# Text exponentials of four heads as one instruction, with subtraction and sum on the vector engine, in a two-layer cross-attention

## The chip, the cores and the metric

The kernel runs on one core of a Trainium2 chip. The metric is the device time of one execution in microseconds (us). The kernel before took 2083.08 us, the median of three runs (2079.56, 2083.08 and 2083.56).

The core's engines are called by the profile's names: PE does matrix products and transposes (PEld is its loading of weights), DVE is the vector engine, ACT the scalar engine (exponentials and scaled copies), POOL the general one, and SP only issues DMA transfers. PE's results land in PSUM, a small memory of banks; the other operands lie in SBUF, the core's working memory.

## The reference, cut to what matters

Two cross-attention layers are computed one after the other. The second takes the first's result as its `x`. Everything is in fp32.

```python
# x: (8, 100, 640); ctx: (8, 722, 1024) = 77 text tokens, then 645 ip tokens; 20 heads of 32
text, ip = ctx[:, :77], ctx[:, 77:]
q = x @ Wq;  k, v = text @ Wk, text @ Wv;  k_ip, v_ip = ip @ Wk_ip, ip @ Wv_ip
# layer 0: attention over the text tokens and, apart from it, over the ip tokens
out = softmax(q k^T * scale) v + softmax(q k_ip^T * scale) v_ip
# layer 1: the ip scores get a term that is the same for all heads, and the ip part a mask by query
text_probs = softmax((q @ k^T over all 640 channels) * scale)
sem = ((text_probs @ text) @ ip^T) * scale
out = softmax(q k^T * scale) v + mask * (softmax(q k_ip^T * scale + 0.5 * sem) v_ip)
# both layers
x = out @ Wo + bo + x
```

There are two softmaxes for each query and head: one over 77 text scores and one over 645 ip scores. The change touches how the first is computed.

## The kernel before, in words

**The first stage (L222 to L407).** It loads x (`xt`, two batches at a time) and the query weights of layer 0 (`wq0`, five pieces of 128 rows) on SP's queue (L227 to L233). It multiplies them (`psq`, L253: four groups of two batches, k outermost, five products of 128x200 for each k; the trace counts two PE instructions for each fp32 product of the code) and then makes the text keys and values of both layers (`text_k`, `text_v`, `text_v_blocks`). These come from a scheme of seven products of half-size blocks for eight (`seven`). It needs sums of blocks of the tokens (`token_sums`: two on DVE at L213 and L214, two on POOL at L215 and L216) and of the weights (`weight_sums`). The tile `s_text` holds the token sums of the text, and `sums` names which block or sum each of the seven products reads. Results go to device memory by DMA on POOL's queue.

**The main stage.** The work is cut into 16 units u (8 batches of layer 0, then 8 of layer 1), taken in pairs. A unit has five chunks c of four heads each; `ORDER` lists the 80 chunks, in the last pair with the two units' chunks mixed. In each chunk PE does, in an order written by hand (`manual_schedule`, the loop at the end of the kernel):

1. the scores against the first 512 keys (`scores`, part 0, L837),
2. transposes j = 0 and 1 of the chunk before (`transposes`, L922), then 2 and 3,
3. the scores against the remaining 210 keys, 133 of ip and 77 of text (part 1),
4. transposes 4 and 5 of the chunk before, then its product with the values (`values`, L944).

Between these stand fillers. They make keys and values of later pairs (`pair_tasks`, `two_chunks`, `fifth_chunk` with products `psk` L669 and `psv` L675), or the output product and layer 1's query product of a finished pair (`out_piece` L752, `q_piece`). `production` puts each filler at a place on a time axis of chunks, from a start and an end (`plan`) and a cost; `spread` levels them; `between` makes all fillers due before a point. Before each small piece, and at each such point, `apart` also pulls one filler forward that would be due within the next 0.4 of a chunk. `fifth[1]` are six half products of three v blocks for the last pair; the plan spreads them from n + 6.9 to n + 8.6, where n = 70 is the first chunk of that pair. At the very end, in chunk 79, `last_out` multiplies the output weights for the last two units (`pso_last`, L804), adds the residual on DVE (L811) and stores.

**The softmax of a chunk (`scores`).** The scores of four heads lie in one PSUM tile `sc`, which has one buffer, so the next scores product waits until all have read it. DVE takes maxima (L846 in layer 0; L853 in layer 1, which adds `sem` and writes the sum to `p`). ACT takes exponentials with the sums of their rows (L861; each is followed by a read of the accumulator). For the text part, `text_maxima` takes the four heads' negated maxima in one DVE instruction (L867), and `text_exponentials` has ACT do one exponential per head over 77 elements, straight from `sc`, with the maximum as bias and the row sum in the accumulator (L875). DVE makes factors (L878 to L883), ACT scales the first 512 columns of p (L889), DVE scales the rest (L893 and L897). The transposes then read p, two at a time, since their PSUM tiles (`ps_pt`, shared with the output products) have two buffers. Copies to SBUF free them: j = 2 and 5 on ACT (L927), the others on DVE (L929).

These steps are put off in a list `later` and emitted one by one between fillers. An entry marked True has to be emitted before the next scores product, because it reads `sc`. The order on the engines other than PE is the scheduler's.

**Small weights.** `load_wo` (L740 to L743) loads five pieces of 320 KB for the output product ("o"), and in layer 0 five more for the query product ("q"), into tiles tagged "wo" with two buffers, on SP's queue. The pieces are used by `out_piece` in the second chunk of the following pair: two ahead of the first transposes, and one at each of the three later places. A load can start when the piece two before it has been used. `out_piece` adds bias and residual on DVE (L757).

Of the kernel before, what the change touches and what calls it, by code (L numbers as in the profile page):

```python
# [9 lines left out]
F32 = mybir.dt.float32  # L10
AF = mybir.ActivationFunctionType
ALU = mybir.AluOpType
AX = mybir.AxisListType

P = 128
B = 8
S = 100
C = 640
CC = 1024
NT = 77  # L20
# [24 lines left out]
def two_layer_xattn(  # L45
# [166 lines left out]
    def token_sums(a11, a12, a21, a22, s1, s2, s3, s4):  # L212
        nc.vector.tensor_tensor(s1, a21, a22, ALU.add)  # L213
        nc.vector.tensor_tensor(s2, s1, a11, ALU.subtract)  # L214
        nc.gpsimd.tensor_tensor(s3, a11, a21, ALU.subtract)  # L215
        nc.gpsimd.tensor_tensor(s4, a12, s2, ALU.subtract)  # L216
        return {1: a11, 2: a12, 3: s4, 4: a22, 5: s1, 6: s2, 7: s3}
# [4 lines left out]
    with ExitStack() as es:  # L222
        fp = es.enter_context(tc.tile_pool(name="first", bufs=1))
        pj.append(es.enter_context(tc.tile_pool(name="ps_first", bufs=6, space=PSUM)))
        xt = fp.tile([P, B, NC_, S], F32, tag="x", name="xt")
        wq0 = []
        nc.sync.dma_start(xt[:, :2], x_t[:, :2])  # L227
        for k in range(NC_):
            t = fp.tile([P, C], F32, tag="wr", name=f"wq0_{k}", bufs=NCC)
            nc.sync.dma_start(t, wq[0][k * P : (k + 1) * P, :])  # L230
            wq0.append(t)
# [15 lines left out]
        for g in range(B // 2):  # L247
# [16 lines left out]
                )  # L264
            nc.gpsimd.dma_start(q_d[0][g], t)

        st = fp.tile([P, 4, HK, TH], F32, tag="s", name="s_text")
        sums = token_sums(
            *(text[:, HK * h : HK * (h + 1), TH * i : TH * (i + 1)] for i in range(2) for h in range(2)),
            *(st[:, i] for i in range(4)),  # L270
        )

        def text_k(l):
            t = fp.tile([P, 2, 512], F32, tag="ev", name=f"kt4_{l}", bufs=2)
# [110 lines left out]
        def sums_of(kind):  # L385
            weight_sums(kind, {"v": HC, "k": 2 * P}[kind], (nc.vector, nc.gpsimd))

        with tc.manual_schedule(engines={mybir.EngineType.PE}):
            sums_of("k")
            text_k(0)  # L390
            load_wk(wkt[1])
            text_v(0)
            sums_of("v")
            load_left(0)
            text_v_blocks(0)
            load_wv(wvt[1])
            sums_of("k")
            text_k(1)
            load_wk(wki[0])
            left_v(0)  # L400
            load_left(1)
            left_text()
            text_v(1)
            sums_of("v")
            text_v_blocks(1)
            sums_of("k")
            left_v(1)  # L407
# [331 lines left out]

    def load_wo(kind, src, g):  # L740
        for c in range(NC_):
            t = wpool.tile([P, NC_, P], F32, tag="wo", name=f"{kind}_{g}_{c}", bufs=2)
            nc.sync.dma_start(t, src.rearrange("(k p) n -> p k n", p=P)[:, :, c * P : (c + 1) * P])  # L743
            wos[kind, g, c] = t

# [52 lines left out]
    def last_out(i, ks_):  # L798
        g = len(PAIRS) - 1
        if ks_[0] == 0:  # L800
            last_ps[i] = product_ps(f"pso_last_{i}")
        for k in ks_:
            for c in range(NC_):
                nc.tensor.matmul(  # L804
                    last_ps[i][:, c * S : (c + 1) * S], lhsT=last_w[c][:, k, :], rhs=hsg[g][:, i, k, :],
                    start=(k == 0 and c == 0), stop=(k == NC_ - 1), skip_group_check=True,
                )
        if ks_[-1] < NC_ - 1:
            return
        r = resg[g][:, i].rearrange("p c s -> p (c s)")  # L810
        nc.vector.tensor_tensor(r, last_ps[i][:, : NC_ * S], r, ALU.add)  # L811
        nc.sync.dma_start(out[LAST[i] % B], resg[g][:, i])
# [14 lines left out]
    def scores(u, c, part):  # L827
# [38 lines left out]
        def text_maxima():  # L866
            nc.vector.tensor_reduce(st[:, 2, :], sc[:S, :, n:KB], AX.X, ALU.max, negate=True)  # L867

            nc.vector.tensor_tensor(lo, st[:, 0, :], st[:, 1, :], ALU.min)
            nc.vector.tensor_tensor(f, lo.unsqueeze(1).to_broadcast([S, 2, 4]), st[:, 0:2, :], ALU.subtract)  # L870

        def text_exponentials():
            nc.scalar.activation(f, f, AF.Exp)
            for i in range(4):
                nc.scalar.activation(  # L875
                    p[:, i, NI:], sc[:S, i, n:KB], AF.Exp, bias=st[:, 2, i : i + 1], accum_out=st[:, 5, i : i + 1]
                )
            nc.vector.tensor_tensor(st[:, 3:5, :], st[:, 3:5, :], f, ALU.mult)  # L878
            nc.vector.tensor_tensor(st[:, 4, :], st[:, 3, :], st[:, 4, :], ALU.add)

# [21 lines left out]
        if part == 0:  # L902
            maxima((0, 1))
            later.append((True, lambda: (exponentials((0, 1)), maxima((2, 3)))))
            later.append((True, lambda: exponentials((2, 3))))
        else:
            maxima((0, 1, 2, 3))
            later.append((True, lambda: (exponentials((0, 1, 2, 3)), text_maxima())))
            later.append((True, text_exponentials))
            later.append((False, lambda: (factors(), scaled((0, 1)), scaled_rest(False))))  # L910
            later.append((False, lambda: (scaled((2, 3)), scaled_rest(True))))

    pts = {}

    def transposes(u, c, j):
        if j == 0:
            emit(len(later))
            pts[u, c] = one.tile([P, 6, 4 * S], F32, tag="pt", name=f"pt_{u}_{c}")
        rows = P if j < 5 else NTAIL
        ps = ps_pt.tile([P, 512], F32, tag="pt", name=f"pspt_{u}_{c}_{j}")  # L920
        for i in range(4):
            nc.tensor.transpose(  # L922
                ps[:rows, i * S : (i + 1) * S], pr[u, c][:, i, j * P : j * P + rows], ident[:S, :S]
            )
        dst, src = pts[u, c][:rows, j, :], ps[:rows, : 4 * S]
        if j % 3 == 2:
            nc.scalar.copy(dst, src)  # L927
        else:
            nc.vector.tensor_copy(dst, src)  # L929
# [27 lines left out]
    def production():  # L957
# [18 lines left out]
        ]  # L976
        plan.append((n - 10 - AHEAD, n + 2.9, by_chunks[0] + by_chunks[1]))
        plan.append((n + 2.9, n + 6.9, fifth[0]))
        plan.append((n + 6.9, n + 8.6, fifth[1]))
        return [task for a, b, tasks in plan for task in spread(a, b, tasks)]  # L980

    def spread(a, b, tasks):
# [91 lines left out]
    with tc.manual_schedule(engines={mybir.EngineType.PE}):  # L1074
# [20 lines left out]
        def apart(until):  # L1095

            while done[0] < len(todo) and todo[done[0]][1] < until and not any(
                t for t, _, _ in todo[mark[0] : done[0]]
            ):
                next_task()  # L1100
            mark[0] = done[0]

        def between(n, a, b, small):

            mark[0] = done[0]
            for i, (_, f) in enumerate(small):
                make(n + a + (b - a) * (i + 1) / (len(small) + 1))
                apart(n + b + 0.4)
                f()
            make(n + b)  # L1110
            apart(n + b + 0.4)

        make(0.0)
        last = None
# [29 lines left out]
            last = (u, c)  # L1144
        last_out(0, [NC_ - 1])
        for j in range(6):
            transposes(*last, j)
        values(*last)
        last_out(1, [NC_ - 1])


# [44 lines left out]
```

## Time and profile before

| what | value |
|---|---|
| median of three runs | 2083.08 us |
| profiled execution, its own time | 2088.13 us |
| profiled execution, its span | 2086.4 us |
| mean clock granted to PE | 0.996 |
| DVE busy, instructions | 988.3 us, 2526 |
| ACT busy, instructions | 862.8 us, 2830 |
| ACT, text exponentials L875: busy, mean of one | 99.5 us, 320 ns |
| ACT, their accumulator reads: busy, mean of one | 64.2 us, 201 ns |

The span runs from the first to the last instruction of the profiled execution; its own time has 1.7 us more around it, and this execution took 5.05 us more than the median. In a list of groups, a row names a line, an engine, an operation, output and inputs, the shape, the count, then busy time and mean duration in ns, then the engine's idle time ahead of it and what ended that. In a timeline, a row gives start and duration of a run of equal instructions, and in brackets how long the engine had been idle and who released it. In a table of windows, each row is a stretch of time with each engine's busy time, PE's granted clock as a share of full speed, the DMA share and GB/s. A busy PE is not a PE at full speed: at half clock it counts as busy too.

### The profile page before, as it was taken

Reading aid. Unit: us, or ns where it says so; the run is one execution under the profiler, and the core shown is the slowest. Engines: PE = TensorE matmul, PEld = TensorE weight load, DVE = VectorE, ACT = ScalarE, POOL = GpSimd, SP = SyncE. Lnnn points to the kernel's source line nnn. Section 1 sums busy time; section 2 is a strip of 40 time slices with the busy share of each in tenths; the row PEclk is TensorE's granted clock in tenths of the full one; section 3 lists DMA queues with packets and bytes.
Section 4 is the critical chain, followed back from the end, with each engine's and each line's share of the span. In section 5 each row is a group of like instructions: output and inputs, shape, how many; then the busy total and the mean of one; then the engine's idle time right before and its main releaser. Section 6 shows DMA issues by size and latency. Waiting matters only on the chain. (4 is left out here: it accounts for less than half of the span.)

```text
span 2086.4 us, 41767 instructions
## 1 busy us (share of the span) xinstructions
PE 2058.5 (99%) x16690; PEld 1641.6 (79%) x16690; DVE 988.3 (47%) x2526; ACT 862.8 (41%) x2830; POOL 379.8 (18%) x409
## 2 busy tenths in 40 slices
PE   8999999999999999999999999999999999999998
PEld 8676787777777777787788877887888778889786
DVE  2111221345554554444464554445455455667565
ACT  1001000245434544344444544445444445566576
POOL 3213211111110111111141111111111113223120
PEclk9999999999999999999999999999999999999999
DMA  9345232323333443352544443353344344545482
GB/s 350 108 134 165 87 87 78 113 75 96 103 99 119 119 118 88 96 162 81 157 121 131 124 117 81 103 156 94 85 112 132 104 122 136 158 119 142 126 227 73
DMA packets 299104, 255.58 MB, mean 123 GB/s; under 512 B 43102, under 2 KB 267794, under 8 KB 298910
## 3 DMA queue, kind: packets, MB, share of 16 engines
q1 hardware_dynamic: 279374, 184.48, 32.6%
q0 software_dynamic: 19536, 68.43, 9.8%
q8 instruction: 132, 2.16, 0.4%
q14 instruction: 62, 0.51, 0.1%
HBM read 183.93 MB, written 68.93 MB: 121 GB/s over the span
## 5 line engine op out<-in xcount | busy, mean ns | idle before, releaser
L861 ACT ACTIVATE p<-sc,st 100x512 f32<-100x512 f32 (+1 forms) x320 | 166.5, 528 | 227.3 <-DVE st L846 227.3
L929 DVE COPY pt<-pspt 128x400 f32<-128x400 f32 x320 | 175.9, 569 | 122.4 <-PE pspt L922 119.4
L861 ACT ACTIVATE p<-p,st 100x512 f32<-100x512 f32 (+1 forms) x320 | 177.0, 555 | 134.9 <-DVE st L853 134.5
L889 ACT ACTIVATE p<-p,st 100x512 f32<-100x512 f32 x320 | 209.6, 714 | 48.6 <-DVE st L883 48.2
L922 PE MATMUL pspt<-ident,p 100*128 100x100 f32 (+1 forms) x1920 | 212.2, 251 | 7.2 <-DVE res L757 2.5
L922 PEld LDWEIGHTS pspt<-ident,p 100*128 100x128 f32 (+1 forms) x1920 | 187.8, 138 | 37.2 <-issue 5.5
L528 PE MATMUL psv_a<-wv,x 128*128 128x397 f32 (+1 forms) x560 | 185.3, 473 | 2.0 <-ACT vo L174 2.0
L927 ACT COPY pt<-pspt 128x400 f32<-128x400 f32 (+1 forms) x160 | 77.9, 487 | 254.8 <-PE pspt L922 254.7
L528 PE MATMUL psv_d<-wv,s 128*128 128x320 f32 (+1 forms) x560 | 174.7, 454 | 0.0
L552 POOL DMA_DIRECT2D v_d<-vo x70 | 39.5, 564 | 723.6 <-DVE gst L520 386.4
L846 DVE TENSOR_REDUCE st<-sc 100x2 f32<-100x1024 f32 (+1 forms) x120 | 126.2, 1052 | 68.2 <-ACT p L861 37.8
L528 PEld LDWEIGHTS psv_a<-wv,x 128*128 128x128 f32 x560 | 103.1, 189 | 65.9 <-issue 9.4
L853 DVE CUSTOM_DVE_ANT_0 p<-sc,sem 100x512 f32<-100x512 f32 (+1 forms) x320 | 139.6, 490 | 25.4 <-PE sc L837 25.3
L528 PEld LDWEIGHTS psv_d<-wv,s 128*128 128x128 f32 x560 | 103.6, 190 | 56.0 <-issue 6.6
L536 PEld LDWEIGHTS psk_a<-x,wk 128*128 128x128 f32 x1120 | 132.3, 191 | 12.7 <-issue 9.4
L837 PE MATMUL sc<-k,q 32*100 32x210 f32 (+1 forms) x1280 | 140.6, 509 | 1.2 <-ACT p L861 0.6
L564 POOL DMA_DIRECT2D k_d<-ko x70 | 58.2, 831 | 448.6 <-DVE ko L200 426.6
L536 PE MATMUL psk_d<-s,wk 128*128 128x128 f32 (+1 forms) x1120 | 139.7, 277 | 0.0
L536 PE MATMUL psk_a<-x,wk 128*128 128x128 f32 (+1 forms) x1120 | 139.1, 277 | 0.0
L536 PEld LDWEIGHTS psk_d<-s,wk 128*128 128x128 f32 x1120 | 131.2, 191 | 8.2 <-issue 3.3
L503 PE MATMUL psk<-x,wk 128*128 128x256 f32 (+1 forms) x560 | 131.6, 383 | 0.0
L503 PEld LDWEIGHTS psk<-x,wk 128*128 128x128 f32 x560 | 102.1, 189 | 23.2 <-issue 7.9
(207 smaller groups left out, 3403.5 us busy)
## 6 DMA issues: line engine op xcount, KB each, us to landing
x<-ip_t SPq DMA_DIRECT2D x84, 512.0 KB
k<-k_d SPq DMA_DIRECT2D x80, 322.5 KB
v<-v_d SPq DMA_DIRECT2D x80, 320.0 KB
v_d<-vo POOLq DMA_DIRECT2D x70, 320.0 KB, 2.6
k_d<-ko POOLq DMA_DIRECT2D x56, 320.0 KB, 6.8
x<-ip_t SPq DMA_DIRECT2D x22, 532.0 KB
o<-wo SPq DMA_DIRECT2D x35, 320.0 KB
q<-wq SPq DMA_DIRECT2D x20, 320.0 KB
```

What stands on the lines that cost most here:

```text
L503: nc.tensor.matmul(ps[:, : 2 * n], lhsT=W["k", 4][:, k, :], rhs=xs[j][:, :, k, :n], start=(k == 0), stop=(k == NCC - 1),)
L528: nc.tensor.matmul(ps[:, :m], lhsT=sums[which][:, k, :P], rhs=w[:, k, :], start=(k == 0 and not go_on), stop=(k == HK - 1), skip_group_che ...
L536: nc.tensor.matmul(ps[:, r * n : (r + 1) * n], lhsT=W["k", WHICH[which]][:, k, r * P : (r + 1) * P], rhs=sums[which][:, k, :], start=(r == ...
L564: nc.gpsimd.dma_start(k_d[u][:, :, n0 : n0 + n], ko[0][:, h, :, :n])
L837: nc.tensor.matmul(sc[:S, i, : k1 - k0], lhsT=qs_[u][rows, c, :], rhs=ks[u, c][rows, k0:k1], start=True, stop=True)
L846: nc.vector.tensor_reduce(st[:, part, heads[0] : heads[-1] + 1], sc[:S, heads[0] : heads[-1] + 1, :n], AX.X, ALU.max, negate=True,)
L853: nc.vector.tensor_tensor_reduce(out=p[:, i, k0 : k0 + n], in0=sc[:S, i, :n], in1=sems[u][:, k0 : k0 + n], scale=-1.0, scalar=3.0e38, op0= ...
L861: nc.scalar.activation(dst, dst if l else sc[:S, i, :n], AF.Exp, bias=st[:, part, i : i + 1], scale=-1.0 if l else 1.0, accum_out=st[:, 3 ...
L889: nc.scalar.activation(p[:, i, :KA], p[:, i, :KA], AF.Copy, scale=mul[:, 0, i : i + 1])
L922: nc.tensor.transpose(ps[:rows, i * S : (i + 1) * S], pr[u, c][:, i, j * P : j * P + rows], ident[:S, :S])
L927: nc.scalar.copy(dst, src)
L929: nc.vector.tensor_copy(dst, src)
```

## The change

1. **Text softmax.** `text_maxima` has one more DVE instruction: it adds the negated maxima to the text scores of the four heads and writes them to `p`. `text_exponentials` is one exponential over the 4 x 77 elements in SBUF, without a sum, and one sum on DVE. Its entry in `later` is False now: it no longer reads `sc`.
2. **Small weights.** The "wo" tiles have three buffers.
3. **Plan of the last products.** `fifth[1]` is spread to n + 8.95. From chunk 76 on, `apart` looks 0.1 of a chunk ahead.
4. **The end.** Transposes j = 0 of the last chunk are copied by ACT. The addition and the store of `last_out` are a function of their own, called after the last transposes in the program's text.
5. **The start.** The first two batches of x are loaded in five pieces (128 x 2 x 100, 100 KB each), each ahead of the query weights of the same k. `s_text` takes the place of `xt`, so the text's token sums, now made after the weight sums, wait for the last `psq` product.

By the instruction order of the two programs, PE's order differs only in the last chunks. The half products of the fifth chunks (`psk`, `psv`) there are, by chunk: before, 3 in chunk 76, 4 in 77 and none in 78; after, 2 in 76, 3 in 77 and 2 in 78. In chunk 76 the first transposes now come before the half product that they stood behind. On SP's queue three "o" loads stand together where two did, and the following two come one place later.

```diff
@@ -222,10 +222,12 @@
     with ExitStack() as es:
         fp = es.enter_context(tc.tile_pool(name="first", bufs=1))
         pj.append(es.enter_context(tc.tile_pool(name="ps_first", bufs=6, space=PSUM)))
-        xt = fp.tile([P, B, NC_, S], F32, tag="x", name="xt")
+        xt = fp.tile([P, 4 * HK * TH], F32, tag="x", name="xt")[:, : B * NC_ * S].rearrange(
+            "p (b k s) -> p b k s", b=B, k=NC_
+        )
         wq0 = []
-        nc.sync.dma_start(xt[:, :2], x_t[:, :2])
         for k in range(NC_):
+            nc.sync.dma_start(xt[:, :2, k], x_t[:, :2, k])
             t = fp.tile([P, C], F32, tag="wr", name=f"wq0_{k}", bufs=NCC)
             nc.sync.dma_start(t, wq[0][k * P : (k + 1) * P, :])
             wq0.append(t)
@@ -264,11 +266,16 @@
                 )
             nc.gpsimd.dma_start(q_d[0][g], t)
 
-        st = fp.tile([P, 4, HK, TH], F32, tag="s", name="s_text")
-        sums = token_sums(
-            *(text[:, HK * h : HK * (h + 1), TH * i : TH * (i + 1)] for i in range(2) for h in range(2)),
-            *(st[:, i] for i in range(4)),
-        )
+        sums = {}
+
+        def text_sums():
+            st = fp.tile([P, 4 * HK * TH], F32, tag="x", name="s_text").rearrange("p (i k n) -> p i k n", i=4, k=HK)
+            sums.update(
+                token_sums(
+                    *(text[:, HK * h : HK * (h + 1), TH * i : TH * (i + 1)] for i in range(2) for h in range(2)),
+                    *(st[:, i] for i in range(4)),
+                )
+            )
 
         def text_k(l):
             t = fp.tile([P, 2, 512], F32, tag="ev", name=f"kt4_{l}", bufs=2)
@@ -387,6 +394,7 @@
 
         with tc.manual_schedule(engines={mybir.EngineType.PE}):
             sums_of("k")
+            text_sums()
             text_k(0)
             load_wk(wkt[1])
             text_v(0)
@@ -739,7 +747,7 @@
 
     def load_wo(kind, src, g):
         for c in range(NC_):
-            t = wpool.tile([P, NC_, P], F32, tag="wo", name=f"{kind}_{g}_{c}", bufs=2)
+            t = wpool.tile([P, NC_, P], F32, tag="wo", name=f"{kind}_{g}_{c}", bufs=3)
             nc.sync.dma_start(t, src.rearrange("(k p) n -> p k n", p=P)[:, :, c * P : (c + 1) * P])
             wos[kind, g, c] = t
 
@@ -805,8 +813,9 @@
                     last_ps[i][:, c * S : (c + 1) * S], lhsT=last_w[c][:, k, :], rhs=hsg[g][:, i, k, :],
                     start=(k == 0 and c == 0), stop=(k == NC_ - 1), skip_group_check=True,
                 )
-        if ks_[-1] < NC_ - 1:
-            return
+
+    def last_out_add(i):
+        g = len(PAIRS) - 1
         r = resg[g][:, i].rearrange("p c s -> p (c s)")
         nc.vector.tensor_tensor(r, last_ps[i][:, : NC_ * S], r, ALU.add)
         nc.sync.dma_start(out[LAST[i] % B], resg[g][:, i])
@@ -866,15 +875,16 @@
         def text_maxima():
             nc.vector.tensor_reduce(st[:, 2, :], sc[:S, :, n:KB], AX.X, ALU.max, negate=True)
 
+            nc.vector.tensor_tensor(
+                p[:, :, NI:], sc[:S, :, n:KB], st[:, 2, :].unsqueeze(2).to_broadcast([S, 4, NT]), ALU.add
+            )
             nc.vector.tensor_tensor(lo, st[:, 0, :], st[:, 1, :], ALU.min)
             nc.vector.tensor_tensor(f, lo.unsqueeze(1).to_broadcast([S, 2, 4]), st[:, 0:2, :], ALU.subtract)
 
         def text_exponentials():
             nc.scalar.activation(f, f, AF.Exp)
-            for i in range(4):
-                nc.scalar.activation(
-                    p[:, i, NI:], sc[:S, i, n:KB], AF.Exp, bias=st[:, 2, i : i + 1], accum_out=st[:, 5, i : i + 1]
-                )
+            nc.scalar.activation(p[:, :, NI:], p[:, :, NI:], AF.Exp)
+            nc.vector.tensor_reduce(st[:, 5, :], p[:, :, NI:], AX.X, ALU.add)
             nc.vector.tensor_tensor(st[:, 3:5, :], st[:, 3:5, :], f, ALU.mult)
             nc.vector.tensor_tensor(st[:, 4, :], st[:, 3, :], st[:, 4, :], ALU.add)
 
@@ -906,13 +916,13 @@
         else:
             maxima((0, 1, 2, 3))
             later.append((True, lambda: (exponentials((0, 1, 2, 3)), text_maxima())))
-            later.append((True, text_exponentials))
+            later.append((False, text_exponentials))
             later.append((False, lambda: (factors(), scaled((0, 1)), scaled_rest(False))))
             later.append((False, lambda: (scaled((2, 3)), scaled_rest(True))))
 
     pts = {}
 
-    def transposes(u, c, j):
+    def transposes(u, c, j, at_end=False):
         if j == 0:
             emit(len(later))
             pts[u, c] = one.tile([P, 6, 4 * S], F32, tag="pt", name=f"pt_{u}_{c}")
@@ -923,7 +933,7 @@
                 ps[:rows, i * S : (i + 1) * S], pr[u, c][:, i, j * P : j * P + rows], ident[:S, :S]
             )
         dst, src = pts[u, c][:rows, j, :], ps[:rows, : 4 * S]
-        if j % 3 == 2:
+        if j % 3 == 2 or at_end and j == 0:
             nc.scalar.copy(dst, src)
         else:
             nc.vector.tensor_copy(dst, src)
@@ -976,7 +986,7 @@
         ]
         plan.append((n - 10 - AHEAD, n + 2.9, by_chunks[0] + by_chunks[1]))
         plan.append((n + 2.9, n + 6.9, fifth[0]))
-        plan.append((n + 6.9, n + 8.6, fifth[1]))
+        plan.append((n + 6.9, n + 8.95, fifth[1]))
         return [task for a, b, tasks in plan for task in spread(a, b, tasks)]
 
     def spread(a, b, tasks):
@@ -1103,12 +1113,13 @@
         def between(n, a, b, small):
 
             mark[0] = done[0]
+            near = 0.4 if n < NC_ * LAST[0] + 6 else 0.1
             for i, (_, f) in enumerate(small):
                 make(n + a + (b - a) * (i + 1) / (len(small) + 1))
-                apart(n + b + 0.4)
+                apart(n + b + near)
                 f()
             make(n + b)
-            apart(n + b + 0.4)
+            apart(n + b + near)
 
         make(0.0)
         last = None
@@ -1144,9 +1155,11 @@
             last = (u, c)
         last_out(0, [NC_ - 1])
         for j in range(6):
-            transposes(*last, j)
+            transposes(*last, j, at_end=True)
+        last_out_add(0)
         values(*last)
         last_out(1, [NC_ - 1])
+        last_out_add(1)
 
 
 # ---- launch: one core; the arrays laid out for the loads, in the types that they come in ----
```

## The prediction, made before the result was known

> **What bounds the kernel now.** I read the page first, then the waits of PE, then windows, then timelines.
>
> ```profile
> span 2086.4 us, 41767 instructions
> ...
> PE 2058.5 (99%) x16690; PEld 1641.6 (79%) x16690; DVE 988.3 (47%) x2526; ACT 862.8 (41%) x2830; POOL 379.8 (18%) x409
> ```
>
> PE never rests for long; DVE and ACT are under half busy. Work taken from or given to DVE and ACT moves the end only where PE waits for it. The waits of PE (total, times, longest):
>
> ```profile
> PE psq L253 <- DMA wq<-wq: 5.6, 1, 5.6
> PE pso L752 <- DMA o<-wo: 3.0, 2, 2.4
> ...
> PE pspt L922 <- DVE pt L929: 2.5, 2, 1.9
> ```
>
> The first is the start. The second is an output weight that came late. The third is the last chunks. The timeline of the second (start, duration, count; the bracket is idle time and releaser):
>
> ```profile
> 1783.25 3.55 PE L752 MATMUL pso<-hs,o 128*128 128x200 f32 x20
> 1785.14 8.33 SPq L743 DMA_DIRECT2D o<-wo  x3
> 1790.30 2.76 PE L752 MATMUL pso<-hs,o 128*128 128x200 f32 x10 [2.42 <-DMA o<-wo]
> ```
>
> Pieces 0 and 1 run together; the weights of piece 2 are issued only at 1785.14, when piece 0 has freed one of two buffers, and land about 5 us later. PE's idle time is not the whole bill (window; PE busy, PEld, DVE, ACT, POOL with instruction counts; PE clock; DMA):
>
> ```profile
> 5.60:9.50 3.90, 3.87 (x12) 3.90 (x13) 0.00 (x0) 0.00 (x0) 0.00 (x0) 1.00 1.04 413
> ...
> 1791.20:1794.60 3.40, 3.40 (x19) 2.90 (x21) 0.48 (x2) 0.49 (x1) 0.72 (x1) 0.51 0.07 20
> ...
> 1948.30:1955.10 6.80, 6.80 (x62) 3.55 (x63) 2.52 (x11) 4.38 (x18) 0.00 (x0) 0.50 0.31 94
> ...
> 2054.10:2060.90 6.80, 6.22 (x73) 3.65 (x65) 4.35 (x20) 4.69 (x20) 0.00 (x0) 0.50 0.15 41
> ```
>
> After each group of stalls the clock is halved for 3.4 or 6.8 us, which loses half of that. At the start twelve instructions take 3.9 us although the clock column shows 1.00: 0.325 us each, where the timeline above has 3.55 / 20 = 0.178. Between 9.5 and 1791.2 the clock is 1.00. The last chunks, each from its first scores product to the next chunk's (76, 77, 78):
>
> ```profile
> 2025.10:2036.12 11.02, 10.69 (x133) 8.81 (x129) 6.75 (x27) 8.57 (x31) 2.14 (x4) 1.00 0.74 186
> 2036.12:2048.54 12.42, 12.42 (x157) 10.97 (x153) 9.39 (x34) 10.61 (x35) 1.07 (x2) 1.00 0.68 191
> 2048.54:2058.83 10.29, 7.63 (x93) 5.15 (x89) 6.72 (x26) 8.55 (x30) 1.07 (x2) 0.77 0.15 46
> ```
>
> Chunk 78 has no filler. Its own PE work at full clock is 4.85 us: scores 1.05 + 0.54, three pairs of transposes at 0.69, values 1.17. It takes 10.29, so 5.4 are lost.
>
> **What the skill says.** TensorE: Matmul & The Clock Gate, "What's actually happening": the clock is full or half, and a free-running window of 3413 ns decides. The trace agrees: stretches of 3.4 and 6.8 us, 0.325 against 0.178 us for an instruction. So a removed stall can return a stretch, and a new one can buy one. Perfetto Trace Analysis, "Identifying the Most-Contended Engine": busy time of matmuls is no measure of how near PE is to its limit. The trace agrees: the half-clock windows count as fully busy. DMA: Bandwidth & Descriptors, "Anatomy of one DMA": about 2.0 us fixed for a transfer (stated for GpSimd's); the weight of 320 KB above took 5 us, so an earlier issue is the cure.
>
> **The text softmax (part 1).** All 80 chunks. The groups by form:
>
> ```profile
> L875 ACT ACTIVATE p<-sc,st 100x77 f32<-100x77 f32 x320 | 99.5, 320 | 19.0 <-DVE st L867 19.0
> ...
> L867 DVE TENSOR_REDUCE st<-sc 100x4 f32<-100x308 f32 x80 | 37.9, 473 | 19.7 <-ACT p L861 19.7
> ...
> L893 DVE TENSOR_TENSOR p<-p,st 100x308 f32<-100x308 f32 x80 | 37.7, 471 | 0.0
> ```
>
> Removed: four exponentials and four accumulator reads a chunk, 1.2 us on ACT (they step by 0.30). Added on ACT: one exponential over 308 elements, not in the trace. ScalarE: Activation LUTs, "What ACT_TABLE_LOAD costs", gives 186 + 0.833 x 308 = 443 ns; scaling L861's (686 - 371) / (512 - 133) = 0.83 ns an element from 320 at 77 gives 512. I take 0.47. Added on DVE: a subtraction of 308 elements from PSUM and a sum of 308; the nearest rows are L867 (473) and L893 (471), so 0.47 each (bounds 0.40 and 0.55). ACT: 80 x (1.2 - 0.47) = 58 us less. DVE: 80 x 0.95 = 76 us more, 51% instead of 47%. Neither is PE time. What counts is the delay from the second scores product to a finished p, 7.85 us before: -0.73 + 0.95 and some 0.1 for two more crossings between engines = +0.35, so 8.2 (bounds 7.6 and 8.7). What hides it: in chunks 0 to 71, p is ready 4 to 13 us before its transposes (one exception, 1.6). In 72 to 75 the margin is 0.5, 1.1, 1.1, 1.8 us, still more than 0.35. In the last four it is nothing to 0.9, and there it is counted below. Were that cover gone everywhere, 80 x 0.35 = 28 us. Queued behind the new DVE work are the copies L929 and the next maxima; in return the scores buffer is free after the subtraction, about 2 us earlier, but PE waited for it only 0.6 + 0.3 us in all. I count 0 (-0.5 to +1).
>
> **The third weight buffer (part 2).** Weight 2 is issued with 0 and 1, a chunk ahead; weight 3 takes the place at 1785.14, lands about 1790.2, and is used after 1794. So both waits go: 3.0 us. On SP the third load passes no more than the loads of that chunk (DMA 42% busy up to there), 320 KB that have a whole chunk to land. What is late next is nothing near: the softmax stays 4 us ahead there. With the stall the half-clock window at 1791.2 should go: 3.4 / 2 = 1.7. Sum -4.7 (bounds -3.0 and -4.7, if no other stall takes it).
>
> **The last chunks (parts 3 and 4).** In the instruction order of the two programs only the PE order of the end differs. A half product of the fifth chunks takes 1.85 us. Before, chunks 76, 77, 78 hold 3, 4, 0 halves; after, 2, 3, 2. From the second scores product PE now does, before it needs that chunk's p: 0.54, transposes 0.69, a half 1.85, values 1.17, scores 1.05, a half 1.85 = 7.15. With p after 8.2 it stalls 1.05.
> 76: 4.85 + 2 x 1.85 = 8.55, + 0.6 surplus as before (11.02 - 10.40), + 0.4 for transposes that now come before the filler = 9.55.
> 77: 4.85 + 3 x 1.85 + 1.05 = 11.45.
> 78: 4.85 + 2 x 1.85 + 1.05, + 0.7 of the waits for copies, of which one DVE wait was 1.9 = 10.3.
> Sum 31.3 against 33.73: -2.4. Chunk 79, 16.71 before, loses its half-clock beginning (-1.0) but stalls 1.2 for p of chunk 78: +0.2. In the tail, with ACT copying the first transposes, the next ones wait less for the copies queued behind the last addition on DVE (0.62 before); I count about half, -0.35. The later halves also write their v blocks later: the last half ends near 2051.5 where it ended at 2047.4. The load of v behind it was issued at 2050.59, 3.2 later; it moves to about 2055, and the second, which waits for the buffer that the values of chunk 78 free, to about 2057. They are wanted near 2071, so 14 us less some 5 for the transfer hide that.
> Sum -2.5 (bounds -7.5, nothing stalls; +1, two new half-clock windows).
>
> **The start (part 5).** First product at 5.63; the first 500 KB of x landed at 4.70, the first weight at 5.50. Now 100 KB + 320 KB stand ahead instead of 820. Packets: x went in 128 of 4000 bytes at 155 ns over 16 DMA engines, 1.24 us; now 256 of 400 bytes. 308-byte packets took 20 ns, 512-byte ones 27, so about 23: 0.37 us. So 0.87 earlier at most. Five more issues on SP at 0.47 us do not bind, since a k step has ten instructions, 3.3 us at half clock and 1.8 at full, and the next piece needs two issues, 0.94. The text's token sums now wait for the last q product, which ends at 41.6 (before, they ran at 17.7 to 26.2): DVE's 2.79 + 1.44 end near 45.9, POOL's last 2.80 near 48.7. The first product that reads them (pskt_b) starts at 51.80 and the last of them is read near 62, so 6 us hide it; without them it would cost up to 4.2. I take -0.7 (-0.3 if the clock rises at 9.5 anyway, to -1.0).
>
> **Sum.** 0 - 4.7 - 2.5 - 0.7 = -7.9: the profiled execution's 2088.13 (span 2086.4) becomes 2080.2. The median shown is 5.05 us below that execution, so it probably has fewer half-clock windows to give back; I count half of the 1.7: -7.05 on 2083.08 = **2076.0**.
>
> **Rivals.** Half-clock windows are luck. *Better* (chance 0.24): the last chunks run without stalls (27.5 + 15.7 instead of 33.73 + 16.71, -7.2, tail -0.35), and the window at 1948 goes as well (-3.4): with 4.7 and 0.7, -16.4 in the profiled execution; less 1.0 in the median, some 2067.7. For: the fillers reach chunk 78. Against: 7.15 is below 8.2.
> *Gain refunded* (0.21): the stalls of 1.05 us in 76 to 79 each buy a window; two cost 3.4 and the last chunks give +1 instead of -2.5; only the idle 3.0 and the start remain: -3.0 - 0.4 + 1 = -2.4 to -3.5, about 2080.
> *Slower* (0.05): the added DVE work sits ahead of L929's copies and of the next maxima, and these are queued behind it. If p comes d later than before, chunks 76 to 79 are each late by d, and 72 to 75 by d less their margins of 0.5, 1.1, 1.1 and 1.8: 8d - 4.5 in all. Saved elsewhere are 3.0 + 1.7 + 0.7 = 5.4. It is slower by over 0.2% (4.2 us) from d = 1.76; at d = 2 it is 11.5 - 5.4 = +6.1, some 2089. Against: DVE gets 0.95 us of work and ACT gives 0.73 back; d = 2 would need each of them twice over.
> *Not as it says* (0.03): three buffers, but SP's queue holds the third load behind others: -2.5 - 0.7, 2079.9. Against: the order on SP shows three weight loads in a row.
>
> **Chances.** Forecast 0.47; with the others 1.00. Faster by over 0.2% (4.2 us, about what a measurement of this kernel can tell from no change; below 2078.9): 0.47 + 0.24 and a little of the refund, 0.73. Within: 0.22. Slower: 0.05. The range, 2067.5 to 2082.5, reaches to the better case and past the refund.
>
> **What would show it.** First PE product near 4.9. No wait of PE on o<-wo, and no half clock around 1791. Chunk 78 still about 10 us long, but with two halves in it and no wait of 1.9. L875's place taken by one exponential of about 0.47, DVE's two new rows at 0.47; p ready 8.2 us after its scores. Wrong if these hold and the median does not fall, or if waits for p appear before chunk 72.

## The result, and the profile after

The changed kernel takes 2072.50 us, the median of six runs (2071.53 to 2073.34). The kernel before takes 2083.44 us beside it (six runs, 2079.56 to 2084.58). The ratio is 0.9949, with a 95% interval of 0.9937 to 0.9962: faster by 0.5%, or 10.9 us. The forecast was 7 us, and its range holds the result.

The page and the waits of PE after the change answer to those shown of before:

```profile
span 2071.1 us, 41271 instructions
...
PE 2051.7 (99%) x16690; PEld 1638.6 (79%) x16690; DVE 1044.4 (50%) x2685; ACT 797.4 (39%) x2271; POOL 381.9 (18%) x409
```

```profile
PE psq L255 <- DMA wq<-wq: 4.6, 1, 4.6
...
PE psv_a L536 <- ACT vo L174: 0.3, 1, 0.3
```

DVE has 56 us more and ACT 65 less, where 76 and 58 were forecast; DVE's two new groups, shown below, are 75.5 us, and others of its groups got shorter. PE's wait for `o<-wo` is gone, and so is the wait of 1.9 us for the copies in chunk 78. The last line is what the prediction had left out. Before, it read

```profile
PE psv_a L528 <- ACT vo L174: 2.0, 1, 2.0
```

and stood at chunk 29. That wait is gone; the 0.3 us that are left stand at chunk 1, where the changed kernel loses 0.4 us.

The last chunks (76, 77, 78), in the columns of the prediction's tables of windows, have no half clock left:

```profile
2013.59:2023.18 9.59, 9.10 (x116) 6.91 (x113) 7.49 (x29) 7.16 (x23) 1.07 (x2) 1.00 0.81 213
2023.18:2033.87 10.69, 10.69 (x141) 9.16 (x137) 8.46 (x32) 8.91 (x26) 1.47 (x3) 1.00 0.75 212
2033.87:2043.93 10.06, 9.05 (x124) 7.32 (x121) 8.15 (x30) 8.51 (x25) 1.74 (x4) 1.00 0.10 31
```

They last 9.59, 10.69 and 10.06 us, where 9.55, 11.45 and 10.3 were forecast and 11.02, 12.42 and 10.29 measured before. Chunk 78 is as long as before, but holds two half products now.

The text softmax, by form:

```profile
L878 DVE TENSOR_TENSOR p<-sc,st 100x308 f32<-100x308 f32 x80 | 38.0, 475 | 0.0
...
L887 DVE TENSOR_REDUCE st<-p 100x4 f32<-100x308 f32 x80 | 37.5, 468 | 12.0 <-ACT p L886 12.0
```

```profile
L886 ACT ACTIVATE p<-p 100x308 f32<-100x308 f32 x80 | 36.7, 458 | 29.7 <-DVE p L878 29.7
```

All three cost what was forecast: 475 and 468 ns on DVE, 458 on ACT.

**Where the time went.** I took the start of each chunk's first scores product in both profiled executions and followed how the difference (after less before) grows. A minus means that the changed kernel gains there.

| place | change in us |
|---|---|
| up to chunk 28 | +0.2 |
| chunk 29 | -2.2 |
| chunk 48, chunks 58 and 59 | -0.6, -0.5 |
| chunk 61 (wait for the weight) | -3.7 |
| chunks 70 and 71 | -3.7 |
| chunks 75 to 78 | -4.1 |
| from the transposes of chunk 79 to the last addition | -0.4 |

With a few tenths elsewhere that is the 15.3 us between the two spans. Not all of it is the change. Half-clock windows of 3.4 and 6.8 us, which cost up to half of their length, account for up to 1.7 us at chunk 61 and up to 3.4 of the 3.7 us at chunks 70 and 71. In chunk 75 PE waited 0.53 us for loads of `x` in the profiled execution of before, and not in a second one of the same kernel (below). The medians are only 10.9 apart: the profiled execution of before had three half-clock windows (mean clock 0.996), and not every execution has them. Beside the experiments, executions of the kernel before ran from 2080.67 us to 2086.72 us, and one of 2080.93 us had a clock of 0.999.

### The profile page after: what moved, and what is told of

The parts are those of the page before. It is cut to its first block, busy times and chain, and to the rows that moved or that the text cites. A ratio compares the mean times of both kernels' runs of the same rounds, so it can differ in the third digit from the quotient of the medians.

```text
span 2071.1 us, 41271 instructions
## 1 busy us (share of the span) xinstructions
PE 2051.7 (99%) x16690; PEld 1638.6 (79%) x16690; DVE 1044.4 (50%) x2685; ACT 797.4 (39%) x2271; POOL 381.9 (18%) x409
## 4 chain that ended last, share of the span: by engine, by line
PE 96%; DVE 2%; ACT 1%; issue 0%; DMA 0%; SPq 0%; DVEq 0%; ACTq 0%
PE psv_a L536 8%; PE psv_d L536 8%; PE pspt L932 8%; PE psk_d L544 6%; PE psk_a L544 6%; PE sc L846 6%; PE psk L511 6%; PE pv L954 4%; PE psv_e L536 4%; PE psv_c L536 4%; PE psv_b L536 4%; PE psk_b L544 3%; PE psk_e L544 3%; PE psk_c L544 3%; PE pso L760 3%; PE psq L255 2%
```

## The experiments

My first theory after the result was that each part has its own place in this table. The softmax would have gained at chunk 29 and in the last chunks, although I had forecast nothing from it. The rival was my forecast: the softmax is worth nothing. Times below are medians with the lowest and highest run; the changed kernel is 2072.50. The kernel before, measured beside the change and beside each group of experiments, had medians of 2083.44 to 2083.93, so half a microsecond of a difference from the changed kernel can come from that alone.

| kernel | us | runs |
|---|---|---|
| changed, two buffers again (`no_third_buffer`) | 2074.66 | 5, 2073.42 to 2076.77 |
| changed, old softmax (`old_softmax`) | 2074.42 | 5, 2073.86 to 2075.93 |
| changed, old plan (`old_plan`) | 2075.09 | 5, 2074.28 to 2077.07 |
| changed, old start (`old_start`) | 2073.16 | 5, 2072.90 to 2073.87 |
| before, new softmax (`only_softmax`) | 2080.02 | 17, 2078.26 to 2084.70 |
| before, three buffers (`only_buffer`) | 2081.35 | 13, 2078.88 to 2083.38 |
| before, new plan (`only_plan`) | 2081.01 | 21, 2078.65 to 2083.08 |
| before, once more (`before_again`) | 2086.36 | 1 |
| changed, four exponentials from SBUF (`four_from_sbuf`) | 2074.41 | 5, 2073.84 to 2075.03 |
| changed, old flag (`flag_true`) | 2072.76 | 5, 2071.24 to 2075.20 |
| changed, old end (`old_end`) | 2074.04 | 5, 2072.31 to 2076.61 |
| changed, idle products at the start (`warm_start`) | 2070.78 | 5, 2070.32 to 2071.60 |

**The changed kernel with one part undone.** Two buffers:

```diff
-name=f"{kind}_{g}_{c}", bufs=3)
+name=f"{kind}_{g}_{c}", bufs=2)
```

> The changed kernel with two buffers for the small weights again. Theory (each part has its own place in the ledger of the two traces; chunk 61 came 3.7 us closer with the third buffer): 2075 to 2077 us, the wait of PE for o<-wo of about 2.4 us is back near chunk 61, with a half-clock window of 3.4 us behind it. Rival (the earlier softmax or other work takes up the stall, the buffer is worth nothing by itself): 2072 to 2073.5 us, and no such wait.

Measured: 2074.66, so +2.2. Its waits of PE and its timeline:

```profile
PE pso L760 <- DMA o<-wo: 3.1, 2, 2.6
```

```profile
1781.37 9.05 SPq L751 DMA_DIRECT2D o<-wo  x3
...
1786.68 3.34 PE L760 MATMUL pso<-hs,o 128*128 128x200 f32 x10 [2.57 <-DMA o<-wo]
```

```profile
1786.10:1789.50 3.40, 2.82 (x9) 2.85 (x10) 0.00 (x0) 0.00 (x0) 0.00 (x0) 0.50 0.17 57
```

The wait is back, with a half-clock window right behind it, at the same chunk, as the theory had it; the median is 0.3 below its interval. In this profiled execution the place costs 4.0 us, and the second wait for a weight, at chunk 71, 0.6; in the median both together cost 2.2.

Old softmax (the subtraction, the one exponential and the sum out, the four exponentials with bias and accumulator in, the flag True):

> The changed kernel with the four text exponentials per chunk on ACT again (and no subtraction and sum on DVE). Theory (the new softmax shortens the chain from scores to p by about 0.45 us and relieves ACT; the waits at chunk 29 and around chunk 70 went for that reason): 2076 to 2081 us, PE's wait for ACT vo at L174 of about 2 us is back at chunk 29, p is ready 7.8 to 7.9 us after the second scores product. Rival (my prediction: the softmax is worth nothing, the chain gets longer by it): 2071 to 2073 us, p ready after 7.4 us or less.

Measured: 2074.42, +1.9, 1.6 below the theory's interval and 1.4 above the rival's. Its waits:

```profile
PE sc L846 <- ACT p L884: 1.9, 4, 0.9
PE psv_a L536 <- ACT vo L174: 1.7, 1, 1.7
```

The wait at chunk 29 is back, and another: the next scores product waits for the exponentials of the text, which free the scores buffer last, 1.9 us in four places (chunks 1, 71, 78 and 79). In the last chunks little of this shows: from the start of chunk 76 to the last chunk's transposes this kernel takes 47.09 us, the changed kernel 46.71.

Old plan:

```diff
-        plan.append((n + 6.9, n + 8.95, fifth[1]))
+        plan.append((n + 6.9, n + 8.6, fifth[1]))
...
-            near = 0.4 if n < NC_ * LAST[0] + 6 else 0.1
+            near = 0.4
```

> The changed kernel with the old plan for the last products (n + 8.6, 0.4 of a chunk ahead throughout). Theory: chunk 78 is without filler again, the last chunks lose 2.5 to 4 us, 2075 to 2076.5 us. Rival (the shorter softmax chain alone mends the last chunks): 2072 to 2073.5 us.

Measured: 2075.09, +2.6. The theory held: chunk 78 is bare again, its transposes wait for the copies, and a long half-clock stretch begins there:

```profile
2040.80 1.60 PE L932 MATMUL pspt<-ident,p 100*128 100x100 f32 x8 [2.12 <-DVE pt L939]
```

```profile
2040.40:2050.60 10.20, 9.22 (x85) 6.27 (x85) 7.03 (x27) 5.81 (x19) 0.00 (x0) 0.50 0.18 51
```

Old start (x of the first two batches in one piece ahead of all weights):

> The changed kernel with the first two batches of x loaded in one piece ahead of the weights, as before. Theory (the time of the first product counts on average, the granting of the full clock comes as much earlier): first product 5.6 us, 2073.5 us. Rival (the earlier start is spent at half clock, and the full clock comes when it comes, as in the two traces): first product 5.6 us, 2072.0 to 2072.8 us.

Measured: 2073.16, +0.7, between the two intervals, with PE's first wait 5.3 us instead of 4.6. The two kernels' runs overlap (2072.90 against 2073.34), so the size is uncertain. In its profile the full clock came at 10.2 us, in the changed kernel's at 10.3; in that pair the earlier start was spent at half clock, as the rival had it. Across the profiled executions, `warm_start` below apart, the full clock came between 7.7 and 11.5 us. So the mean gain can be near the theory's while one pair shows none; which of the two holds is not settled.

**The kernel before with one part alone.** First the kernel before itself, for a second profile.

> The kernel before, once more, for a second profile. Theory (the places of the stalls are fixed, the half-clock windows behind them are chance): PE waits for o<-wo at chunk 61 (about 2.4 us) and for ACT vo (about 2.0 us) at chunk 29 again, but the half-clock windows after 1780 us differ in number or place from those at 1791, 1948 and 2054, and the span is 2080 to 2084 us. Rival (the windows belong to the places): the same three windows within 1 us, span within 1 us of 2086.4.

Measured: span 2084.6 us, between the two theories' figures. PE waits at chunk 29 (1.7 us) and for `o<-wo` (1.8 at most) again. Two of the half-clock windows are back at the same chunks (they start at 1946.9 and 2052.7 us, where the whole program is 1.3 us earlier), the one behind chunk 61 is not. So both theories were half right: a place makes a window likely, and does not decide it. The other profiles say the same. Five of them have the wait at chunk 61; where it was 2.4 to 2.6 us (the kernel before, `no_third_buffer`, `only_softmax`) a window of 3.4 us followed, where it was 1.7 or 1.8 (this one and `only_plan`) none did. Five have the old plan; in four of them a window begins at chunk 78, in `only_softmax` none does.

New softmax alone:

> The kernel before with the new text softmax alone (one exponential of four heads, subtraction and sum on DVE). Theory: PE's wait of 2.0 us at chunk 29 goes, p is ready 0.4 to 0.5 us earlier, the last four chunks gain some of it; 2079.5 to 2081.5 us. Rival (my prediction: worth nothing by itself): 2083 to 2084.5 us.

Measured: 2080.02 against 2083.93 of before on the same chip, -3.9; the ratio of the runs is 0.9984 (0.9977 to 0.9991). The gain at chunk 29 is there at its full size (2.2 us). My forecast of nothing falls.

Three buffers alone. For the room that they need, `s_text` takes the place of `xt`, so this kernel has that part of the change too:

> The kernel before with three buffers for the small weights alone; for the room they need, the text's token sums take the place of x, as in the changed kernel. Theory: both waits of PE for o<-wo go, 3.0 us and a part of a half-clock window; 2079 to 2081 us. Rival (the stall moves to the next late thing): 2082.5 to 2084.5 us.

Measured: 2081.35, -2.6; ratio 0.9988 (0.9980 to 0.9997), above the theory's interval by 0.35 and clear of the rival's. Both waits for `o<-wo` are gone.

New plan alone:

> The kernel before with the new plan for the last products alone (n + 8.95 and 0.1 of a chunk). Theory: chunk 78 gets two half products, 2080 to 2082 us. Rival (the plan needs the shorter softmax chain; with the old one the fillers only move the waits for p): 2083 to 2084.5 us.

Measured: 2081.01, -2.9; ratio 0.9986 (0.9980 to 0.9993). The plan does not need the new softmax, though with the old one the scores product waits for L875 in chunks 1, 71, 78 and 79 (1.9 us in all).

The parts alone sum to 3.9 + 2.6 + 2.9 = 9.4; the same three undone to 1.9 + 2.2 + 2.6 = 6.7. The whole is 10.9, with the start and the end in it.

**What in the softmax gains.** The new softmax shortens the steps on ACT, frees the scores buffer earlier, and emits its exponential later. Two kernels take these apart.

```diff
-            nc.scalar.activation(p[:, :, NI:], p[:, :, NI:], AF.Exp)
-            nc.vector.tensor_reduce(st[:, 5, :], p[:, :, NI:], AX.X, ALU.add)
+            for i in range(4):
+                nc.scalar.activation(p[:, i, NI:], p[:, i, NI:], AF.Exp, accum_out=st[:, 5, i : i + 1])
```

> The changed kernel with the subtraction on DVE, but four exponentials of 77 elements in SBUF with their sums in the accumulator instead of one exponential and a sum on DVE. Theory (the gain of the softmax is the shorter chain, from fewer instructions on ACT): p is ready about 0.4 us later than in the changed kernel, the last four chunks lose about that each, PE's wait at chunk 29 may come back; 2073.5 to 2075.5 us. Rival (the gain is the scores buffer that is free earlier, and the subtraction's place): 2072.3 to 2073 us.

Measured: 2074.41, +1.9. In chunks 73 and 74, p is ready 7.64 and 7.65 us after the second scores product, against 7.36 and 7.35 in the changed kernel and 7.89 in the kernel before. The wait at chunk 29 is back:

```profile
PE psv_a L536 <- ACT vo L174: 1.9, 1, 1.9
```

The program comes 2.2 us later by it, and another 1.05 at chunks 48, 58 and 59. The scores buffer is freed by the subtraction as in the changed kernel, so the rival falls: nearly all that the softmax gains in the median needs the single exponential with its sum on DVE. The median lies in the theory's interval, but not for the theory's reason: from the start of chunk 76 to the last chunk's transposes this kernel takes 46.64 us against 46.71, so the later p costs nothing in the last chunks.

```diff
-            later.append((False, text_exponentials))
+            later.append((True, text_exponentials))
```

> The changed kernel with the text exponential emitted before the next scores product again (its entry in the list of put-off steps True). Theory (the chain sets the gain, not the order in which the steps are put off): 2072.2 to 2073 us. Rival (the later emission gives ACT and DVE room for what PE waits for): 2073.5 to 2075 us.

Measured: 2072.76 (2071.24 to 2075.20). The order in which the steps are put off is worth nothing that shows.

**Chunk 29, closer.** The timelines around PE's wait, of the kernel before:

```profile
1060.16 1.43 POOL L216 TENSOR_TENSOR s<-x,s 128x512 f32<-128x512 f32 x1
1060.20 4.26 DVE L897 TENSOR_TENSOR p<-p,st 100x532 f32<-100x532 f32 x1
...
1061.40 2.48 POOL L132 TENSOR_TENSOR wkt<-wk,wk 128x1024 f32<-128x1024 f32 x1
...
1064.56 1.21 DVE L846 TENSOR_REDUCE st<-sc 100x2 f32<-100x1024 f32 x1
```

and of the changed kernel:

```profile
1059.89 1.57 POOL L216 TENSOR_TENSOR s<-x,s 128x512 f32<-128x512 f32 x1
...
1060.24 1.79 DVE L907 TENSOR_TENSOR p<-p,st 100x532 f32<-100x532 f32 x1
...
1061.88 2.38 POOL L132 TENSOR_TENSOR wkt<-wk,wk 128x1024 f32<-128x1024 f32 x1 [0.41 <-DMA wk<-wki]
...
1062.13 1.21 DVE L855 TENSOR_REDUCE st<-sc 100x2 f32<-100x1024 f32 x1
```

No shorter chain gained here: after the second scores product of chunk 28, the reciprocal comes 0.2 us later in the changed kernel than in `old_softmax`. DVE scales a part of p (L897 before, L907 after), which takes 0.70 us in 78 of the 80 chunks of the kernel before and in 77 of the changed kernel. At this place it takes 4.26 us before, and ends 0.57 us after the second of two POOL instructions that stand back to back; in the changed kernel it takes 1.79 and ends 0.57 us after the first. Behind it wait the next maxima, behind these on ACT the exponentials, behind those the copy of `vo` (L174), and for that PE waits. The Trainium skill, SBUF — State Buffer, "SBUF: two separate sides", says that DVE instructions with two SBUF inputs and GpSimd's that read SBUF share a pair of ports, that whoever starts first holds it for the whole instruction, and that the other is blocked. These durations agree.

All fourteen profiles fall into two groups. The instruction took 4.26 to 4.29 us in the six with four text exponentials (the kernel before twice, `old_softmax`, `only_buffer`, `only_plan`, `four_from_sbuf`), and 1.79 or 1.80 in the eight with one. In the six it starts 0.03 or 0.04 us after POOL's L216, in the eight 0.35 us after. So it belongs to the softmax, but as a matter of three tenths of a microsecond in the order of DVE and POOL. A gap behind L216 is not what decides: in the profile shown, POOL waited 0.41 us for a load, in `no_third_buffer` the gap is 0.08 us, in `old_start` and `flag_true` there is none, and all four have the short time. No run shifted POOL or DVE by itself. That the order sets the duration therefore rests on these fourteen profiles, and why the blocked instruction lets a second one pass in the one order only stays open.

**The end and the start.** Without the copy on ACT:

```diff
-        if j % 3 == 2 or at_end and j == 0:
+        if j % 3 == 2:
```

> The changed kernel with the last chunk's first transposes copied by DVE again. Theory (my prediction's term): 0.35 us more, 2072.8 to 2073 us, with DVE's copy of j = 0 behind the last addition. Rival (the wait moves to the next copy): 2072.5 us.

Measured: 2074.04, above both intervals, with a wide spread (2072.31 to 2076.61). The three slowest of its five runs have a mean clock of 0.997 or 0.998, so half-clock windows, which its profiled execution (2072.31) does not have before the end; whether the old end brings them on is open. So the median does not settle 0.35 us. The profiles do: from the transposes of chunk 79 to the start of the last addition it takes 6.99 us here and in the kernel before, 6.56 in the changed kernel, and PE's wait of 0.62 us for DVE's copies is back. The term is 0.43.

The first q products run at half clock for 5.7 us in the changed kernel. The last experiment keeps PE busy before they can start:

```diff
+        zero = fp.tile([P, 64], F32, tag="evl", name="zero", bufs=1)
+        nc.vector.memset(zero, 0.0)
+        idle = product_ps("idle")
+        for _ in range(22):
+            nc.tensor.matmul(idle[:64, :64], lhsT=zero, rhs=zero, start=True, stop=True)
```

> The changed kernel with 22 products of zeros (64x64x64, results unread) ahead of the first loads' use, so that PE is busy from about 1 us on. Theory (PE's clock rises a fixed stretch after its work begins; in the changed kernel 5.7 us of q products ran at half clock): full clock about 3 us earlier, 1 to 2 us saved, 2070.5 to 2071.5 us. Rival (the rise depends on the moment alone, or idle products do not count): first product at 4.6 us or later, 2072.3 to 2073 us.

Measured: 2070.78 (2070.32 to 2071.60), 1.7 us less than the changed kernel (2071.53 to 2073.34) and 0.9939 (0.9926 to 0.9951) of the kernel before. Its timeline:

```profile
1.02 4.00 PE L229 MATMUL idle<-zero 128*64 128x64 f32 x44 [1.02 <-DVE zero L226]
...
4.95 9.23 PE L260 MATMUL psq<-xt,wq 128*128 128x200 f32 x53
```

The full clock came at 3.7 us, and the program is 2.4 us earlier in that execution. The first q product starts 0.4 later (4.95 against 4.59), so 22 products are probably a few too many.

## Why the prediction was right, and where its terms were off

**The sign and the range held.** The sum in the median was -7.05; measured -10.9. All of the -7.05 stood for the buffer, the end and the start, which are worth about 2.6 (buffer) and 2.9 (plan) by the medians of one part alone, 0.4 (copy at the end) by the profiles and 0.7 (start): 6.6 together. The rest is in the main the softmax, put at nothing. That the range held the result all the same is owed to its width, and in this part to luck.

- *Third buffer: -4.7 in the profiled execution, -3.85 in the median.* The mechanism held. In the profiles the place gained 3.7 us, and with the buffer taken out again chunks 61 and 71 lost 4.6, near the forecast; in the medians it is 2.2 to 2.6. The clock part was taken too high for the median: the second profile of the kernel before has the wait, 1.8 us, and no half clock behind it.
- *Last chunks: -2.5.* Measured -3.4 in chunks 76 to 78, -0.35 in chunk 79 (16.71 to 16.36), -0.43 in the tail, all in the profiles; by the median of the plan alone -2.9. The halves stand where the instruction order said. What was too dear were the stalls of 1.05 us, since p comes after 7.55 to 7.8 us in these chunks and not after 8.2; and no new half-clock window came, which was the risk in *Gain refunded*. The window at 1948 went as well, as *Better* had it.
- *Start: -0.7.* First product at 4.59 instead of 5.63, more than forecast (near 4.9). Undoing it costs 0.7 in the median.
- *Text softmax: "I count 0 (-0.5 to +1)".* This step failed. The softmax is worth -3.9 alone, and +1.9 when it is taken out, outside these bounds.

**The failed step.** I let the softmax reach PE by one path only, "the delay from the second scores product to a finished p", and wrote for it "-0.73 + 0.95 and some 0.1 for two more crossings between engines = +0.35". The size was right in layer 0 and wrong where it counted, and PE's gain did not come by this path.

*The size.* Against `old_softmax`, which differs in the softmax alone, p is ready 0.32 us later on average in layer 0 (chunks 0 to 39), as reckoned, and later in 32 of these 40 chunks; nearly all of it is hidden. There the subtraction is on the path: ACT's exponential waits for it in 29 of the 40 chunks, as in chunk 28:

```profile
1055.71 0.46 ACT L886 ACTIVATE p<-p 100x308 f32<-100x308 f32 x1 [1.03 <-DVE p L878]
```

In layer 1 it waits for it in no chunk, and p comes 0.04 us earlier on average. The timeline of chunk 74 after:

```profile
1996.99 0.48 DVE L878 TENSOR_TENSOR p<-sc,st 100x308 f32<-100x308 f32 x1
1997.04 0.18 ACT L870 ACTIVATION_READ_ACCUMULATOR p<-p,st 100x1 f32 x1
1997.13 0.39 ACT L870 ACTIVATE p<-p,st 100x133 f32<-100x133 f32 x1
...
1997.83 0.47 ACT L886 ACTIVATE p<-p 100x308 f32<-100x308 f32 x1
...
1998.40 0.46 DVE L887 TENSOR_REDUCE st<-p 100x4 f32<-100x308 f32 x1
...
1999.16 0.20 DVE L892 RECIPROCAL st<-st 100x8 f32<-100x8 f32 x1
```

DVE subtracts while ACT still has the last of the ip exponentials to do. From the second scores product (1994.93) the reciprocal comes after 4.23 us. In the kernel before it came after 4.77: 2005.75 to

```profile
2010.28 0.20 ACT L875 ACTIVATION_READ_ACCUMULATOR p<-sc,st 100x1 f32 x1
2010.52 0.20 DVE L882 RECIPROCAL st<-st 100x8 f32<-100x8 f32 x1 [0.94 <-ACT p L875]
```

The text exponentials end 1.4 us earlier (3.37 after the scores product instead of 4.73), and the sum and the small steps behind it give 0.8 of that back. So the chain is 0.54 shorter, not 0.35 longer, in chunks 73 and 74. In the last four chunks p is ready between 0.23 us earlier and 0.08 later than in `old_softmax`, so nothing was lost there by the added work.

*The path.* In the profiles the largest gain of the softmax, 2.2 us, lies at chunk 29, in layer 0, where the steps from scores to the reciprocal take longer than with the old softmax. By the profiles it came by DVE's long instruction, the maxima behind it and the copy of `vo`. The next, 1.05 us at chunks 48, 58 and 59, is no matter of an earlier p either, which is 0.5 and 0.2 us later in the first two. The last chunks gained 0.4.

**What the prediction did not see.** The list of waits before had PE's wait of 2.0 us for `vo`, and I passed over it. The softmax removed it, as far as the profiles show, by a shift of POOL against DVE, which I would not have found from the sum of durations. The gain of 3.7 us at chunks 70 and 71 belongs to no single part: no kernel with one part undone brought more than 0.6 of it back. That place had a half-clock window in both profiles of the kernel before and in none of the kernels with any part changed. Each part alone takes something from the stalls in front of it or moves it in time; which of these prevents the window stays open.

## What to carry to other kernels

Before putting a new instruction's duration on a chain, ask in each stage which engine ends last at its place in the timeline. The same subtraction was off the path in layer 1 and on it in 29 of the 40 chunks of layer 0. Then ask what else the engine's new order moves: here the largest gain lay with an instruction outside the chain. Read every line of the list of waits of the bounding engine, also the single ones far from the change, and look for an instruction there that is several times longer than its kind. Where PE is the bound, look at its first microseconds too: here 5.7 us of its first products ran at half clock, and keeping it busy from 1.02 us on saved 1.7 us.

## What was not expected of the hardware

One DVE instruction with two SBUF inputs, 0.70 us long elsewhere, took 4.26 to 4.29 us when it started 0.03 or 0.04 us after a POOL instruction that another one followed, and 1.79 or 1.80 when it started 0.35 us after the same one. Products of zeros, 2.7 us of them, were enough for the full clock at 3.7 us in one execution, where it came between 7.7 and 11.5 us without them. At chunk 61 a wait of PE of 2.4 to 2.6 us was followed by 3.4 us at half clock in three executions, and one of 1.7 or 1.8 us by none in two.
